# Pre-layernorm attention with a quantised linear layer: the first layernorm moved to other places and turned by VectorE and DMAs

## The chip, the cores and the metric

The kernel runs on one NeuronCore of a Trainium2 chip. Five engines with queues of their own share the work: PE (TensorE, matrix products and transposes, results in PSUM), DVE (VectorE), ACT (ScalarE), POOL (GpSimd) and SP (SyncE, which here only issues DMAs). Every DMA of the kernel is issued on SP's queue. The metric is the device time of one execution in microseconds, lower is better. The kernel before takes 774.85 us, the median of three runs (774.77 to 775.24).

## The reference, cut to what matters

There are 16 sequences of 256 tokens with 256 features, all float32. For each sequence:

```python
def layernorm(x):  # over the features, no scale, no shift
    return (x - mean(x)) / sqrt(var(x) + 1e-5)

h = layernorm(x)                      # "first layernorm"
q, k, v = h @ wq.T, h @ wk.T, h @ wv.T   # 16 query heads, 4 key/value heads, width 128
s = q @ k.T / sqrt(128)               # masked: a window of 32 and 4 sink tokens
x = x + softmax(s) @ v @ wo.T
h = layernorm(x)                      # "second layernorm"
hq = clip(round(h / scale), -128, 127)   # scale = max|h| / 127 for each token
x = x + (hq @ weight_q.T) * scale * weight_scale + bias
```

Matrix products need the features of `h` on the partitions, and the layernorm leaves the tokens there. So both layernorms are followed by a transpose.

## The kernel before, in words

**Slots.** The attention is cut into 128 units `(n, g, t)`: sequence, key/value head (with its four query heads), half of the tokens. The main loop goes over slots, one unit in each and two more at the end; eight slots make a sequence (`PER`). In a slot, PE makes the scores of the slot's unit (`pss`, L527), part of the output projection of an earlier unit (`py`, L645), the weighted values of the unit two slots back (`po`, L590), in every other slot a quarter of the next sequence's keys or values (`pk`, `pv`), and a pair of its query heads (`pq`, L494). Products of blocks are made with seven instead of eight matmuls, so sums of blocks are needed as factors: `os` of the attention's output and `xs` of the turned layernorm, both on POOL. Slots are named below by their place in a sequence: slot s is s modulo 8.

**Order.** The order in which instructions stand on each engine is the order in which the program writes them (`in_written_order`, L21). Small steps are hung on slots with `at(slot, f)` (L790) and run at the end of their slot. An instruction whose input is late thus holds back all that is written behind it on its engine, SP's DMA queue included.

**Weights of the attention.** After the softmax, VectorE turns the weights in blocks of 32 by 32 (`z`, L549), a DMA writes them to DRAM (`zd`, L551), and at the start of the next slot another brings them back in the wanted order (`ad`, L555); `po` two slots after the unit reads them. So `ad` has a little over one slot to be issued and to land.

**First layernorm.** `norm_steps` (L357) has three steps: statistics (`statistics`, L178: two instructions per half on DVE, two small ones on POOL, L187 and L188), and the two halves of the standardisation (L193, DVE). Then `turned` (L368) makes four PE transposes of 128x128 into PSUM (`xt`, L373), a DVE copy to `xnT` (L374), and POOL's four sums `xs` (`right_sums`, L263 to L266). Lines 807 to 813 hang these on four consecutive slots: statistics in slot 6, halves in slots 7 and 0, `turned` in slot 1, which is seven slots before the sequence begins; its `x` is loaded in slot 4. The first sequence has a function of its own, the second uses early slots.

**Second layernorm.** `ffn_steps` (L662) has six steps: `stats`, `norm` (with the bias added to x on POOL), `scale`, `quantise`, `turn` (a DMA transpose to `hT`, L695) and `linear` (four bf16 matmuls, L708; DVE scaling, L713; POOL addition, L714; the output's DMA, L715). They sit in slots 4, 5, 6, 0, 1 and 2 after their sequence (L834 to L840). The last but one sequence has them in slots 4 to 9 of the last sequence (the last two of these slots come after the last unit), and adds its bias inside `linear`. The last sequence is finished by `last_steps(0)` and `last_steps(1)` (L719), a half of the tokens each, at the very end.

**Values.** `values_to` (L412) lays values out for the window in one of three buffers, taken in rotation (L406 to L410).

**Weights.** Sums of blocks of the output weights (`output_weight_sums`, POOL) are made in slots 9 to 12 of the first two sequences, and the steps that quantise the linear layer's weights (`ffn_weight_steps`) in slots 5, 6, 8, 9, 10 and 11.

Of the kernel before, what the change touches and what calls it, by code (L numbers as in the profile page):

```python
# [9 lines left out]
FP = mybir.dt.float32  # L10
BF = mybir.dt.bfloat16
# [23 lines left out]
def kernel(  # L35
# [12 lines left out]
    pe, dve, act, pool, sp = nc.tensor, nc.vector, nc.scalar, nc.gpsimd, nc.sync  # L48
    B, T, DM = x.shape
    P = 128  # L50
    D = 128
# [3 lines left out]
    NC = DM // P  # L55
    NT = T // P
# [4 lines left out]
    QB = 32  # L61
    NBLK = P // QB
    SB = T // QB
# [5 lines left out]
    NKP = NCH * QB  # L69
# [1 line left out]
    SCALE = 1.0 / math.sqrt(D)  # L71

    const = ctx.enter_context(tc.tile_pool(name="const", bufs=1))
    xp = ctx.enter_context(tc.tile_pool(name="xp", bufs=4))
    p1 = ctx.enter_context(tc.tile_pool(name="p1", bufs=1))
    p2 = ctx.enter_context(tc.tile_pool(name="p2", bufs=2))
    p3 = ctx.enter_context(tc.tile_pool(name="p3", bufs=3))
    dram = ctx.enter_context(tc.tile_pool(name="dram", bufs=3, space=bass.MemoryType.DRAM))
# [12 lines left out]
    def load_x(n):  # L91
        if n < B:
            xts[n] = xp.tile([P, NT, DM], FP, tag="x", name=f"x_{n}")
            sp.dma_start(xts[n], x_v[n])
# [16 lines left out]
    bias_bc = const.tile([P, DM], FP, name="bias_bc")  # L111
# [138 lines left out]
    def fast_queries(n, h=0):  # L250
        return n > 0 and (n, h) != (B - 1, H - 2)
# [10 lines left out]
    def right_sums(t, b11, b12, b21, b22):  # L262
        pool.tensor_sub(t[0], b12, b11)  # L263
        pool.tensor_sub(t[1], b22, t[0])
        pool.tensor_sub(t[2], b22, b12)
        pool.tensor_sub(t[3], b21, t[1])  # L266
# [67 lines left out]
    xns, xnT, qt, kt, vw, xn_sums, mvs = {}, {}, {}, {}, {}, {}, {}  # L334
# [19 lines left out]
    def xn_blocks(n):  # L354
        return [[xnT[n][:, c, j * P : (j + 1) * P] for j in range(NT)] for c in range(NC)]

    def norm_steps(n):  # L357
# [7 lines left out]

        return [stats, lambda: norm(0), lambda: norm(1)]

    def turned(n):  # L368
        xnT[n] = p2.tile([P, NC, T], FP, tag="xnT", name=f"xnT_{n}")
        pt = ps_m.tile([P, NC, T], FP, tag="m", name=f"xt_{n}")  # L370
        for c in range(NC):
            for j in range(NT):
                pe.transpose(pt[:, c, j * P : (j + 1) * P], xns[n][:, j, c * P : (c + 1) * P], ident)  # L373
        dve.tensor_copy(xnT[n], pt)  # L374
        if fast_queries(n):
            xn_sums[n] = p2.tile([P, 4, P], FP, tag="xs4", name=f"xs4_{n}")
            b = xn_blocks(n)
            right_sums([xn_sums[n][:, i] for i in range(4)], *b[0], *b[1])

    def first_sequence():  # L380

# [22 lines left out]

    vws = [const.tile([NKP, SB, 2 * D], FP, name=f"vw_{j}") for j in range(3)]

    def values_buffer(n, pair):
        vw[n, pair] = vws[(2 * n + pair) % 3]  # L410

    def values_to(n, pair, v, tiles=range(NT)):  # L412


        w, fresh = vw[n, pair], 2 * n + pair < 3
        b0, b1 = tiles[0] * NBLK, (tiles[-1] + 1) * NBLK
        sp.dma_start(w[1:NKP:NCH, b0:b1], v[b0:b1].rearrange("b k d -> k b d"))
        c1 = min(b1 + 1, SB)
        sp.dma_start(w[0:NKP:NCH, b0 + 1 : c1], v[b0 : c1 - 1].rearrange("b k d -> k b d"))
        if b0 == 0:  # L420
            rows = QB if fresh else SINK
            sp.dma_start(w[2 : NCH * (rows - 1) + 3 : NCH], v[0, 0:rows].unsqueeze(1).to_broadcast([rows, SB, 2 * D]))
            if fresh:
                sp.dma_start(w[0:NKP:NCH, 0], v[0])
# [189 lines left out]
    def output_weight_sums(g):  # L614
        t = [wo_sums[:, i, 2 * g : 2 * g + 2] for i in range(4)]
        right_sums(t, *(wo_half(g, p, half) for p in range(2) for half in range(2)))
# [45 lines left out]
    def ffn_steps(n):  # L662
        xt = xts[n]
        tiles, tag = range(NT), f"{n}"
        h = p1.tile([P, NT, DM], FP, tag="h", name=f"h_{tag}")
        h16 = p1.tile([P, NT, DM], BF, tag="h16", name=f"h16_{tag}")
        xs = p2.tile([P, NT], FP, tag="xs", name=f"xs_{tag}")
        hT = p1.tile([P, NT, NC, P], BF, tag="hT", name=f"hT_{tag}")
        y = p1.tile([P, NT, DM], FP, tag="yo", name=f"y_{tag}")
        got = []  # L670

        def stats():
            got.append(statistics(xt, tiles, f"f{tag}"))

        def norm():
            standardise(h, xt, got[0], tiles)
            if n < B - 2:
                add_bias()

        def scale():  # L680
            dve.tensor_reduce(xs, h, AX.X, ALU.max, apply_absolute_value=True)
            dve.tensor_scalar(xs, xs, 1.0 / 127.0, 1e-12, ALU.mult, ALU.max)

        def quantise():
            xr = p2.tile([P, NT], FP, tag="xr", name=f"xr_{tag}")
            dve.reciprocal(xr, xs)
            for j in tiles:
                dve.scalar_tensor_tensor(
                    h[:, j, :], h[:, j, :], xr[:, j : j + 1], magic.to_broadcast([P, DM]), ALU.mult, ALU.add
                )  # L690
            pool.tensor_scalar(h, h, MAGIC + 127.0, MAGIC - 128.0, ALU.min, ALU.max)
            pool.tensor_scalar(h16, h, MAGIC, None, ALU.subtract)

        def turn():
            sp.dma_start_transpose(  # L695
                hT.rearrange("p j c t -> p (j c) t"), h16.rearrange("p j d -> p (j d)")
            )

        def add_bias():
            pool.tensor_add(xt, xt, bias_bc.unsqueeze(1).to_broadcast([P, NT, DM]))  # L700

        def linear():
            if n == B - 2:
                add_bias()
            pa = ps_m.tile([P, NT, DM], FP, tag="m", name=f"pa_{tag}")
            for j in tiles:
                for c in range(NC):
                    pe.matmul(  # L708
                        pa[:, j, :], hT[:, j, c], wqfT[:, c, :],
                        start=(c == 0), stop=(c == NC - 1),  # L710
                    )
            for j in tiles:
                dve.scalar_tensor_tensor(y[:, j, :], pa[:, j, :], xs[:, j : j + 1], wsc_bc, ALU.mult, ALU.mult)  # L713
            pool.tensor_add(y, y, xt)  # L714
            sp.dma_start(out_v[n], y)  # L715

        return [stats, norm, scale, quantise, turn, linear]

    def last_steps(j):  # L719

# [2 lines left out]
        n, tag = B - 1, f"last_{j}"  # L723
# [3 lines left out]
        y = p1.tile([P, NT, DM], FP, tag="xn", name=f"y_{tag}")[:, 0]  # L727
        mv = p2.tile([P, nc.vector.BN_AGGR_DIM], FP, tag="mv2", name=f"mv_{tag}")
        top, by, xs, least = (p2.tile([P, 1], FP, tag=k, name=f"{k}_{tag}") for k in ("top", "by", "xs1", "least"))
        hT = p1.tile([P, NT, NC, P], BF, tag="hT", name=f"hT_{tag}")[:, 0]  # L730

        def stats():
            st = p2.tile([P, nc.vector.BN_STATS_DIM], FP, tag="st2", name=f"st_{tag}")
# [45 lines left out]
    PER = G * NT  # L779
# [5 lines left out]
    def lag(i):  # L785
        return 2 if FIRST <= i < TAIL else 1

    chunks, early, asked, shares, small = {}, {}, {}, {}, {}

    def at(slot, f, what=small):  # L790
        what.setdefault(slot, []).append(f)
# [13 lines left out]
        for slot, h in zip(q, range(0, H, 2)):  # L805
            at(n * PER + slot, (n, h), asked)
    for n in range(1, B):
        first = n * PER - 10
        places = (first, first + 1, first + 2, first + 3) if n > 1 else (0, 1, 1, 2)
        for k, slot in enumerate(places[:3]):  # L810
            at(slot, lambda n=n, k=k: norm_steps(n)[k]())
        at(places[3], lambda n=n: turned(n))
        at(max(first - 2, 0), lambda n=n: n > 1 and load_x(n))
    for i, (n, g, t) in enumerate(units):
        if n == 0:
            at(i + 2 + lag(i), lambda u=(n, g, t): projected(*u), shares)
# [8 lines left out]
    at(1, lambda: weight_sums(wk_sb, wk_sums))  # L825
    for g in range(G):
        at((2, 4, 6, 8)[g], lambda g=g: weight_sums(wq_sb[:, :, g * HG * D : (g + 1) * HG * D], wq_sums[:, g]))
        at(9 + g, lambda g=g: output_weight_sums(g))
    at(0, other_loads)
    for slot, f in zip((5, 6, 8, 9, 10, 11), ffn_weight_steps()):  # L830
        at(slot, f)
    steps = {}
    for n in range(B - 1):
        done = (n + 1) * PER  # L834
        for k, slot in enumerate((4, 5, 6, 8, 9, 10) if n < B - 2 else (4, 5, 6, 7, 8, 9)):
            def step(n=n, k=k):
                if k == 0:
                    steps[n] = ffn_steps(n)
                steps[n][k]()
            at(done + slot, step)  # L840


    warm = ps_m.tile([P, P], FP, tag="m", name="warm")
# [14 lines left out]
    def get(i):  # L858
        return units[i] if 0 <= i < len(units) else None

    waiting, later, ways = None, {}, {}
    def values_now(i):
        return [times_values(*units[j]) for j in (i - 2, i - 1) if get(j) and j + lag(j) == i]

    def small_steps(i):
        for f in small.pop(i, []):
            f()

    for i in range(len(units) + 2):
        if i > len(units):  # L870
            small_steps(i)
        u, w = get(i), get(i - 1) if lag(i - 1) == 1 else None
        chunk = chunks.pop(i, [None])[0]
        nmax = scores_and_turned(u, w)
        if i - 1 in ways:
            ways.pop(i - 1)()
        if waiting:
            waiting.first()
        shared = shares.pop(i, [])
# [11 lines left out]
        waiting = None  # L891
# [33 lines left out]
        for f in combined:  # L925
            if f:
                f()
        if i == len(units) - 1:
            tail = last_steps(0)
            for f in tail[:2]:  # L930
                f()
# [38 lines left out]
```

## Time and profile before

| What | Value |
|---|---|
| runs | 774.85, 775.24, 774.77 us |
| the profiled execution: its own time | 774.85 us |
| its span (first to last instruction) | 773.1 us |
| time outside the span | 1.75 us |
| mean granted TensorE clock | 0.996 |
| busy: PE / DVE / POOL / ACT | 760.6 / 617.5 / 511.2 / 399.2 us |
| PE's transposes for the first layernorm (L373) | 60 matmuls, 9.0 us busy, 15 sequences |
| DVE's copies behind them (L374) | 15, 692 ns each |

Times in the profile are microseconds from the span's start, `x8` is a number of instructions, and brackets give the idle time ahead of an instruction and what ended it. Neighbouring matmuls overlap, so PE's busy time is no measure of a matmul's cost; the distance from one group's start to the next is. `PEld` is the load of the stationary operand, `SPq` the issue of a DMA.

### The profile page before, as it was taken

To read this page: it belongs to the slowest core of one execution; us is meant where nothing else is said; L and a number is where in the kernel's file an instruction comes from. 1 tells how busy PE (TensorE), PEld (TensorE's weight loads), DVE (VectorE), ACT (ScalarE), POOL (GpSimd) and SP (SyncE) were. 2 spreads that over 40 slices of the span, in tenths; PEclk is the share of its full clock that TensorE was granted. 3 is DMA by queue.
4 is the path that set the end of the run, shared out by engine and by line. 5 is a ranking of instruction groups with operands and counts; after the bars stand their busy time and mean duration, and the time that the engine had idled before them with its cause. 6 is when DMAs were issued, how large, how long until landed. Compare 5 with 4: busy or idle time off the path is not lost.

```text
span 773.1 us, 18754 instructions
## 1 busy us (share of the span) xinstructions
PE 760.6 (98%) x6539; PEld 748.1 (97%) x6539; DVE 617.5 (80%) x1774; ACT 399.2 (52%) x1561; POOL 511.2 (66%) x813
## 2 busy tenths in 40 slices
PE   9999999999999999999999999999999999999995
PEld 7999999999999999999999999999999999999993
DVE  2577888888888888888888888888888878878766
ACT  3655455455455454545555455554545555455551
POOL 4667967776765866767676666767667677676614
PEclk9999999999999999999999999999999999999998
DMA  7634334334343334434334343334434334343311
GB/s 243 197 100 113 120 110 124 105 95 137 118 138 109 106 103 120 141 113 123 101 96 141 110 141 105 104 115 120 130 114 127 97 106 141 103 134 105 99 35 34
DMA packets 113329, 90.34 MB, mean 117 GB/s; under 512 B 14548, under 2 KB 111444, under 8 KB 113236
## 3 DMA queue, kind: packets, MB, share of 16 engines
q1 hardware_dynamic: 113236, 89.16, 37.8%
q8 instruction: 52, 0.85, 0.5%
q14 instruction: 41, 0.34, 0.1%
HBM read 50.99 MB, written 36.18 MB: 113 GB/s over the span
## 4 chain that ended last, share of the span: by engine, by line
PE 95%; DVE 3%; ACT 0%; issue 0%; POOL 0%; DVEq 0%; POOLq 0%; ACTq 0%
PE pq L494 24%; PE py L645 23%; PE po L590 14%; PE pss L527 14%; PE pk L464 6%; PE pv L474 6%; PE py L629 3%; PE pq L505 2%; PE pa L708 1%; PE xt L373 1%; PE warm L845 1%; PE pv L439 0%; PE pk L430 0%; PE ptd L532 0%; ACT scores L565 0%
## 5 line engine op out<-in xcount | busy, mean ns | idle before, releaser
L565 ACT ACTIVATE scores<-scores,nmax 128x68 f32<-128x68 f32 x512 | 173.5, 340 | 254.3 <-DVE nmax L540 251.5
L590 PE MATMUL po<-ad,vw 96*128 96x128 f32 x1024 | 135.5, 275 | 0.0
L527 PE MATMUL pss<-kt,qt 128*128 128x68 f32 x1024 | 130.2, 268 | 0.0
L590 PEld LDWEIGHTS po<-ad,vw 96*128 96x128 f32 x1024 | 125.4, 192 | 1.6 <-ACT ad L535 0.7
L527 PEld LDWEIGHTS pss<-kt,qt 128*128 128x128 f32 x1024 | 126.1, 192 | 0.7 <-issue 0.5
L494 PE MATMUL pq<-xs,wq_sums 128*128 128x128 f32 x714 | 118.6, 275 | 0.0
L538 DVE SCALAR_TENSOR_TENSOR scores<-pss,masks 128x272 f32<-128x272 f32 x128 | 56.3, 440 | 67.7 <-PE pss L527 66.2
L494 PEld LDWEIGHTS pq<-xs,wq_sums 128*128 128x128 f32 x714 | 98.8, 192 | 0.0
L565 ACT ACTIVATION_READ_ACCUMULATOR scores<-scores,nmax 128x1 f32 x512 | 95.6, 187 | 0.0
L602 ACT COPY oT<-po 128x512 f32<-128x512 f32 x129 | 75.4, 585 | 22.6 <-PE po L590 22.6
L645 PE MATMUL py<-wo_sums,os 128*128 128x128 f32 x672 | 87.0, 279 | 0.0
L645 PEld LDWEIGHTS py<-wo_sums,os 128*128 128x128 f32 x672 | 79.5, 192 | 0.0
L304 POOL TENSOR_TENSOR ktmp<-b_k 128x256 f32<-128x256 f32 x30 | 24.6, 820 | 83.0 <-ACT b_k L325 83.0
L549 DVE STREAM_TRANSPOSE z<-scores 128x384 f32<-128x384 f32 x120 | 69.4, 578 | 4.1
L494 PE MATMUL pq<-xnT,wq_sb 128*128 128x128 f32 x476 | 72.6, 275 | 0.0
L257 POOL TENSOR_TENSOR os<-oT 128x256 f32<-128x256 f32 x56 | 41.2, 735 | 47.4 <-ACT oT L602 47.4
L494 PEld LDWEIGHTS pq<-xnT,wq_sb 128*128 128x128 f32 x476 | 62.7, 192 | 0.0
L645 PE MATMUL py<-wo_sb,oT 128*128 128x128 f32 x448 | 62.0, 281 | 0.0
L304 POOL TENSOR_TENSOR vt<-b_v 128x256 f32<-128x256 f32 x30 | 21.9, 729 | 57.8 <-ACT b_v L325 57.8
L540 DVE TENSOR_REDUCE nmax<-scores 128x4 f32<-128x272 f32 x128 | 55.8, 436 | 4.4
L584 DVE TENSOR_TENSOR scores<-scores,sm 128x272 f32<-128x272 f32 x120 | 55.2, 460 | 4.1
L645 PEld LDWEIGHTS py<-wo_sb,oT 128*128 128x128 f32 x448 | 54.5, 192 | 0.0
(184 smaller groups left out, 1740.9 us busy)
## 6 DMA issues: line engine op xcount, KB each, us to landing
zd<-z SPq DMA_DIRECT2D x120, 192.0 KB
ad<-zd SPq DMA_DIRECT2D x120, 192.0 KB
vw<-vd SPq DMA_DIRECT2D x31, 256.0 KB
vd<-vt SPq DMA_DIRECT2D x30, 256.0 KB
vw<-vd SPq DMA_DIRECT2D x30, 224.0 KB
x<-in_x_dram SPq DMA_DIRECT2D x15, 256.0 KB
out_dram<-y SPq DMA_DIRECT2D x15, 256.0 KB
wq_sb<-in_wqT_dram SPq DMA_DIRECT2D x4, 512.0 KB
```

The costliest lines, as they stand in the source:

```text
L304: eng.tensor_add(c11_u, like(p[0][:, 0:2], c11_u), two(p1, c11_u))
L464: pe.matmul(to, left, right, start=True, stop=True)
L494: pe.matmul(to, left, right, start=True, stop=True)
L527: pe.matmul(pss[:, k, :], qt[n, g][:, t, k].rearrange("p h i -> p (h i)"), kt[n, g][:, t * NBLK + k, :], start=True, stop=True,)
L538: dve.scalar_tensor_tensor(s[:, :, 0:NK], pss, SCALE, masks[:, t], ALU.mult, ALU.add)
L540: dve.tensor_reduce(nmax, s[:, :, 0:NK], AX.X, ALU.max, negate=True)
L549: dve.transpose(z, s.rearrange("p k (c i) -> p c k i", c=NCH))
L565: act.activation(s[:, k, 0:NK], s[:, k, 0:NK], AF.Exp, bias=nmax[:, k : k + 1], scale=1.0, accum_out=sm[:, k : k + 1],)
L584: dve.tensor_mul(s, s, sm.unsqueeze(2).to_broadcast([P, NBLK, NK]))
L590: pe.matmul(po[:, k], vw[n, g // 2][:, t * NBLK + k, g % 2 * D : (g % 2 + 1) * D], ad[:, :, k], start=True, stop=True,)
L602: act.copy(o[:, t, hs].rearrange("p h (k i) -> p k h i", i=QB), po[:, :, hs])
L645: pe.matmul(region(py, i), left[:, e], right[:, e], start=(g == 0 and e == 0 and i in (1, 4)), stop=(g == G - 1 and e == 1 and i in (7, 3)),)
```

## The change

1. **First layernorm, from the third sequence on.** The PE transposes are replaced by `turned_by_blocks`: DVE turns all 32x32 blocks in one instruction (128x512), four DMAs write the blocks to DRAM in pieces of 512 bytes (`out`), and four more bring them back to `xnT` in pieces of 128 bytes (`back`). POOL's sums become a function of their own (`channels`). The second sequence keeps `turned`.
2. **Places.** Statistics move from slot 6 to slot 2, the halves from slots 7 and 0 to slots 4 and 6, the DVE transpose comes in slot 7, `out` in slot 0 and `back` in slot 1, right after `ad` (the new list `begin`), and the sums at the end of slot 1, as before. The third sequence uses slots 4 to 9. `x` is loaded in slot 0, four slots earlier than before, and has five buffers instead of four.
3. **Last but one sequence.** `quantise` joins `scale` in the seventh slot of the last sequence, and its DMA transpose, bias (now on DVE) and `linear` all come in the eighth: the transpose at its start, `linear` just ahead of the first part of `last_steps(0)` (the new list `close`). `last_steps` takes its turned tile from two buffers of its own, and the extra call of the small steps in the slots after the last unit goes.
4. **Values.** Two buffers, one for each pair of heads, instead of three in rotation.
5. **Weights.** The last block sum of the output weights moves from slot 12 to slot 14; the linear layer's weight steps to slots 6, 9, 10, 10, 11 and 12.

```diff
-    xp = ctx.enter_context(tc.tile_pool(name="xp", bufs=4))
+    xp = ctx.enter_context(tc.tile_pool(name="xp", bufs=5))
...
+    def channels(n):
+        xn_sums[n] = p2.tile([P, 4, P], FP, tag="xs4", name=f"xs4_{n}")
+        b = xn_blocks(n)
+        right_sums([xn_sums[n][:, i] for i in range(4)], *b[0], *b[1])
...
+    def turned_by_blocks(n):
+        z = p1.tile([P, NQ, NT * NC, QB], FP, tag="zx", name=f"zx_{n}")
+        dve.transpose(z, xns[n].rearrange("p t (c q i) -> p q (t c) i", c=NC, q=NQ))
+        zd = dram.tile([P, NQ, NT * NC, QB], FP, tag="zx", name=f"zxd_{n}")
+
+        def out():
+            for a in range(NQ):
+                sp.dma_start(
+                    zd[:, a].rearrange("(q j) k i -> j q (k i)", q=NQ),
+                    z[a * QB : (a + 1) * QB].rearrange("j q k i -> j q (k i)"),
+                )
+
+        def back():
+            xnT[n] = p2.tile([P, NC, T], FP, tag="xnT", name=f"xnT_{n}")
+            for t in range(NT):
+                for c in range(NC):
+                    sp.dma_start(
+                        xnT[n][:, c, t * P : (t + 1) * P].rearrange("p (a i) -> p a i", a=NQ), zd[:, :, t * NC + c]
+                    )
+
+        return out, back
...
-    vws = [const.tile([NKP, SB, 2 * D], FP, name=f"vw_{j}") for j in range(3)]
+    vws = [const.tile([NKP, SB, 2 * D], FP, name=f"vw_{j}") for j in range(2)]
...
-        vw[n, pair] = vws[(2 * n + pair) % 3]
+        vw[n, pair] = vws[pair]
...
-        return [stats, norm, scale, quantise, turn, linear]
+        return [stats, norm, scale, quantise, turn, linear, lambda: add_bias(dve)]
...
-        hT = p1.tile([P, NT, NC, P], BF, tag="hT", name=f"hT_{tag}")[:, 0]
+        hT = p2.tile([P, NC, P], BF, tag="hT1", name=f"hT_{tag}")
...
-        first = n * PER - 10
-        places = (first, first + 1, first + 2, first + 3) if n > 1 else (0, 1, 1, 2)
+        first = n * PER - 14
+        places = (0, 1, 1, 2) if n == 1 else (4, 5, 6, 7) if n == 2 else (first, first + 2, first + 4, first + 5)
...
+            def turn(n=n, slot=places[3]):
+                for k, f in enumerate(turned_by_blocks(n)):
+                    at(slot + 1 + k, f, begin)
+                at(slot + 2, lambda: channels(n))
...
-        at(9 + g, lambda g=g: output_weight_sums(g))
+        at((9, 10, 11, 14)[g], lambda g=g: output_weight_sums(g))
...
-    for slot, f in zip((5, 6, 8, 9, 10, 11), ffn_weight_steps()):
+    for slot, f in zip((6, 9, 10, 10, 11, 12), ffn_weight_steps()):
...
-        for k, slot in enumerate((4, 5, 6, 8, 9, 10) if n < B - 2 else (4, 5, 6, 7, 8, 9)):
+        slots = (4, 5, 6, 8, 9, 10) if n < B - 2 else (4, 5, 6, 6, 7, 7, 7)
+        for k, slot in enumerate(slots):
...
-            at(done + slot, step)
+            at(done + slot, step, begin if k == 4 and n == B - 2 else close if k == 5 and n == B - 2 else small)
```

More of the change, by code (lines that the diff above doesn't have):

```diff
@@ L374, in turned @@
         dve.tensor_copy(xnT[n], pt)
[L375 to L378, printed above, removed]
+        channels(n)
+    def turned_by_blocks(n):
[16 more added lines that the diff above has]
+        return out, back
+    NQ = P // QB
     def first_sequence():
@@ L402, in keys_to @@
         act.copy(k[:, :, :, 2 * QB :], kb[:, :, 0, 0:SINK].unsqueeze(2).to_broadcast([P, 2, SB, SINK]))
-    vws = [const.tile([NKP, SB, 2 * D], FP, name=f"vw_{j}") for j in range(3)]
+    vws = [const.tile([NKP, SB, 2 * D], FP, name=f"vw_{j}") for j in range(2)]
     def values_buffer(n, pair):
-        vw[n, pair] = vws[(2 * n + pair) % 3]
+        vw[n, pair] = vws[pair]
     def values_to(n, pair, v, tiles=range(NT)):
-        w, fresh = vw[n, pair], 2 * n + pair < 3
+        w, fresh = vw[n, pair], n == 0
         b0, b1 = tiles[0] * NBLK, (tiles[-1] + 1) * NBLK
@@ L677, in norm @@
             if n < B - 2:
-                add_bias()
+                add_bias(pool)
         def scale():
@@ L697, in turn, with add_bias @@
             )
-        def add_bias():
-            pool.tensor_add(xt, xt, bias_bc.unsqueeze(1).to_broadcast([P, NT, DM]))
+        def add_bias(eng):
+            eng.tensor_add(xt, xt, bias_bc.unsqueeze(1).to_broadcast([P, NT, DM]))
         def linear():
-            if n == B - 2:
-                add_bias()
             pa = ps_m.tile([P, NT, DM], FP, tag="m", name=f"pa_{tag}")
@@ L786, in lag @@
         return 2 if FIRST <= i < TAIL else 1
-    chunks, early, asked, shares, small = {}, {}, {}, {}, {}
+    begin, close, chunks, early, asked, shares, small, later = {}, {}, {}, {}, {}, {}, {}, {}
     def at(slot, f, what=small):
@@ L807 @@
     for n in range(1, B):
-        first = n * PER - 10
-        places = (first, first + 1, first + 2, first + 3) if n > 1 else (0, 1, 1, 2)
+        first = n * PER - 14
+        places = (0, 1, 1, 2) if n == 1 else (4, 5, 6, 7) if n == 2 else (first, first + 2, first + 4, first + 5)
         for k, slot in enumerate(places[:3]):
             at(slot, lambda n=n, k=k: norm_steps(n)[k]())
-        at(places[3], lambda n=n: turned(n))
-        at(max(first - 2, 0), lambda n=n: n > 1 and load_x(n))
+        if n == 1:
+            at(places[3], lambda n=n: turned(n))
+        else:
+            def turn(n=n, slot=places[3]):
+                for k, f in enumerate(turned_by_blocks(n)):
+                    at(slot + 1 + k, f, begin)
+                at(slot + 2, lambda: channels(n))
+            at(places[3], turn)
+            at(max(first - 2, 0), lambda n=n: load_x(n))
     for i, (n, g, t) in enumerate(units):
@@ L859, in get @@
         return units[i] if 0 <= i < len(units) else None
-    waiting, later, ways = None, {}, {}
+    waiting, ways = None, {}
     def values_now(i):
@@ L869 @@
     for i in range(len(units) + 2):
-        if i > len(units):
-            small_steps(i)
         u, w = get(i), get(i - 1) if lag(i - 1) == 1 else None
@@ L876 @@
             ways.pop(i - 1)()
+        for f in begin.pop(i, []):
+            f()
         if waiting:
@@ L928 @@
         if i == len(units) - 1:
+            for f in close.pop(i):
+                f()
             tail = last_steps(0)
```

## The prediction

> **What bounds the kernel now.** I read the shares of the engines, then the chain of waits, then PE's idle time by stage, then PE, DVE, POOL and SP row by row in one sequence from the middle. First the page's engine line, the chain's shares and windows of the start, the middle and the end (columns: window, length, busy PE, PEld, DVE, ACT, POOL, granted clock, DMA share, GB/s).
>
> ```profile
> PE 760.6 (98%) x6539; PEld 748.1 (97%) x6539; DVE 617.5 (80%) x1774; ACT 399.2 (52%) x1561; POOL 511.2 (66%) x813
> ...
> PE 95%; DVE 3%; ACT 0%; issue 0%; POOL 0%; DVEq 0%; POOLq 0%; ACTq 0%
> ...
> 95.00:142.00 47.00, 45.67 (x409) 45.43 (x408) 39.59 (x115) 24.48 (x97) 32.86 (x51) 1.00 0.37 113
> 420.00:467.00 47.00, 47.00 (x423) 46.91 (x421) 39.46 (x115) 24.93 (x99) 32.41 (x50) 1.00 0.38 116
> 734.00:773.00 39.00, 30.19 (x192) 26.03 (x191) 25.34 (x73) 13.67 (x48) 10.45 (x17) 0.92 0.13 36
> ```
>
> The reader is to see that PE has no gap in the middle at a full clock, 1.33 us of gap in the window from 95, and 9 us at the end. So in the middle, time goes only if PE work goes, and comes if something makes PE wait. A sequence takes 46.55 us (`py` of the same slot: 404.72, 451.26, 497.82). In the sequence used below, slot 0 starts at 478.30, slot 1 at 484.55, slot 2 at 490.12, slot 3 at 496.81, slot 4 at 501.95 (first `pss`).
>
> **The change part by part.** *PE's transposes.* On PE's timeline:
>
> ```profile
> 489.46 0.39 PE L494 MATMUL pq<-xnT,wq_sums 128*128 128x128 f32 x2
> 489.69 0.60 PE L373 MATMUL xt<-ident,xn 128*128 128x128 f32 x4
> 490.12 1.01 PE L527 MATMUL pss<-kt,qt 128*128 128x68 f32 x8
> ```
>
> From the start of `xt` to the next group's start are 0.43 us. Fourteen of the 15 sequences lose it: 14 x 0.43 = **-6.0 us**, all on the path.
>
> *VectorE.* The copy of 0.69 us goes from slot 1; the transpose of 128x512 comes in slot 7, by the row nearest to it (`z`, a transpose of 128x384 in 0.578) an estimated 0.578 x 512/384 = 0.77. There a half of the standardisation (0.39) leaves, so DVE gets 0.38 more against 0.86 idle ahead of L538. Slot 4 receives a half (0.39, idle 1.15), slot 2 the statistics (0.92, idle 1.64). Nothing reaches PE: 0, and were one cover gone, at most the excess over its idle time, which no row shows.
>
> *A stall at the start goes.* PE waits 1.33 us at 97.56 for DVE's `qt`. DVE stood at `h` (idle 1.12, then 1.60 busy) for POOL's `mv_f`, and POOL made the last block sum of the output weights first (90.08 to 93.2):
>
> ```profile
> 92.26 0.93 POOL L266 TENSOR_TENSOR wo_sums<-wo_sb,wo_sums 128x256 f32<-128x256 f32 x1
> 93.28 0.22 POOL L187 TENSOR_SCALAR mv_f<-mv_f 128x2 f32<-128x2 f32 x1
> 94.33 1.60 DVE L193 TENSOR_SCALAR h<-x,mv_f 128x256 f32<-128x256 f32 x2 [1.12 <-POOL mv_f L188]
> 97.56 0.46 PE L474 MATMUL pv<-wv_sb,xs 128*128 128x128 f32 x2 [1.33 <-DVE qt L305]
> ```
>
> That sum (3.1) moves to slot 14; a weight step (0.61) and a sequence's statistics (0.99) come onto POOL ahead instead. So `mv_f` ends some 3.1 - 1.6 = 1.5 us earlier, before DVE is free for `h` at 93.22. The 1.12 leave DVE, and **-1.2 us** on PE (bounds -1.33 and 0, if another wait takes its place). The remaining 0.81 us stall of the start (slot 6, at 48.68) has none of these instructions before it and stays.
>
> *What the moved statistics delay.* They issue two POOL instructions, 0.22 at L187 and 0.71 at L188; with the 0.06 between, 0.99 us. In slot 2 POOL has them now ahead of the addition that ends the second layernorm's product, L714. Behind L714 stands the output's DMA on SP's queue, and behind that `ad` of slot 3:
>
> ```profile
> 498.66 1.27 POOL L714 TENSOR_TENSOR y<-y,x 128x512 f32<-128x512 f32 x1
> ...
> 521.98 0.22 POOL L187 TENSOR_SCALAR mv_a<-mv_a 128x2 f32<-128x2 f32 x1
> 522.28 0.71 POOL L188 TENSOR_TENSOR mv_a<-mv_a,half 128x2 f32<-128x2 f32 x1
> ...
> 498.73 0.37 SPq L479 DMA_DIRECT2D vd<-vt  x1
> 499.95 0.39 SPq L715 DMA_DIRECT2D out_dram<-y  x1
> 500.45 0.41 SPq L555 DMA_DIRECT2D ad<-zd  x1
> ...
> 504.07 0.97 PEld L590 LDWEIGHTS po<-ad,vw 96*128 96x128 f32 x8
> ```
>
> SP issues `out_dram` when the addition ends, `ad` 0.50 later, `ad` lands at 503.23 (the last completion in the trace), and PE loads its first block at 504.07: 0.84 us of slack. Over the twelve sequences from the third to the fourteenth the slacks are 0.97, 1.03, 0.96, 1.10, 1.02, 0.81, 0.89, 1.00, 0.84, 1.01, 0.81 and 0.59. An `ad` that came just in time showed 0.10 between landing and load. So each sequence loses 0.99 + 0.10 minus its slack, in sum **+2.1 us**. Bounds: 0 (slot 2 starts 0.43 earlier after its neighbour's transposes went, and if POOL runs ahead of PE by that much all of it is covered) and +6 (0.50 in each, the worst slack every time).
>
> *SP's queue and `back`.* In slot 0 SP issues four `out` behind `vw` and `ad`, at 0.60 each by the `vw` rows, so the next `zd` moves from 483.32 to about 484.5 and slot 1's `ad` from 485.26 to about 486.4; its slack in the other sequences is 1.7 to 1.9, so 0.6 remain. Then come the four `back`: 2048 pieces of 128 bytes, 128 for each of the 16 rings. They start when `ad`'s packets end, at about 488.6. No row has pieces of data that small. The two nearest: `hT` moves 256-byte pieces at 24 ns each on a ring (512 of them in 0.78 us), and `ad` 512-byte pieces from DRAM at 46 to 48 (384 in 1.1 to 1.2). So `back` takes 3.1 to 6.1 us and has landed (0.4 for the completion) between 492.1 and 495.1. Then POOL makes the sums `xs`:
>
> ```profile
> 492.23 0.47 POOL L263 TENSOR_TENSOR xs<-xnT 128x128 f32<-128x128 f32 x1
> 495.68 0.73 POOL L304 TENSOR_TENSOR vt<-b_v 128x256 f32<-128x256 f32 x1 [1.62 <-ACT b_v L325]
> ```
>
> The four last 1.84 us. Behind them on POOL stands the combination of the values, L304, which can start at 495.25 (0.43 earlier, as PE). So `back` may land until 493.4 at no cost, which is 34 ns a piece. I take 24: a packet's own duration goes down with its size in this trace (27 ns for 512 bytes, 18 for 256, 9 for 4), so 128 bytes stand nearer to the 256-byte row: **0**. At 48 it would be 495.1 + 1.84 - 495.25 = 1.7 us a sequence.
>
> The Trainium skill speaks against this: its page "DMA: Bandwidth & Descriptors", section Specifications, gives 512 B as the smallest transfer at line rate, with a read-modify-write below. In this trace the 256-byte pieces were quicker than the 512-byte ones; no run shows 128. If the rule doubled the slower pitch, an estimate by that page is 12 us for `back`, and a sum of 769.0 + 12 x 7.9, about 864 us.
>
> *Loads and buffers.* With two value buffers the writer must wait for the product that read them one sequence before, three slots earlier: 0. `x` has one buffer more for a load four slots earlier: 0. The third sequence's `x` now stands ahead of the output weights; their first quarter, landed at 30.48, comes 0.75 to 1.1 later, against PE's need at 32.0: 0. If one of these were not covered it would cost its lateness once, under 1.
>
> *The end.* On DVE and PE:
>
> ```profile
> 762.24 0.87 DVE L713 SCALAR_TENSOR_TENSOR y<-pa,xs,wsc_bc 128x256 f32<-128x256 f32 x2
> 762.38 1.03 PE L629 MATMUL py<-wo_sb,oT 128*128 128x256 f32 x4
> 763.53 1.25 DVE L766 TENSOR_TENSOR y_last<-y_last,x_last 128x256 f32<-128x256 f32 x1
> 764.71 0.42 DVE L734 BATCH_NORM_STATS2 st_last<-py 128x6 f32<-128x256 f32 x1
> ```
>
> The last half's statistics start at 764.71 though their `py` ended at 763.41: DVE was busy with L713 and with L766, which took 1.25 where its twin later takes 0.42, with POOL's L714 running. After the change L713 and L714 come before `last_steps(0)`. Its statistics go from 756.45 to about 757.8, its `d_last` ends at 761.6 instead of 760.6, the last `py` at 763.87 (+0.46), L766 takes 0.42, and the last half's statistics start at 764.0: **-0.7 us**. Bounds: -1.3 (they start as `py` ends, as before) and +1.33 (the shift of the first half passes through whole).
>
> *Sum.* 774.85 (the profiled execution; 773.1 of span and 1.75 around it; it is also the median of the runs) - 6.0 - 1.2 + 2.1 - 0.7 = **769.0 us**.
>
> **The rivals.** *A, `ad` isn't late.* POOL waits for ACT and PE in slots 1 and 2 (1.62 idle ahead of L304), so it may regain the 0.43 in each sequence; against it, 18.0 us of SP's idle time end on this very addition. 769.0 - 2.1 = 766.9. *B, slower: `back` is too slow.* POOL's `xs` come late, the value combination behind them, `vd`, `out_dram` and `ad` behind it, with no slack left. From 34 ns a piece each further ns costs 128 x 0.001 x 12 = 1.5 us; break-even with before at 38; at `ad`'s 48 the time is 769.0 + 12 x 1.7 = 789.4. For it: `ad` also comes from DRAM, and its 46 ns are more than its packets' own 27. Against it: `hT`. *C, the end gets longer.* The path from L713 over the first half's statistics holds the end as a whole: +1.33 instead of -0.7, 771.0.
>
> **How the numbers follow.** Forecast 0.52, A 0.16, C 0.08, B 0.24. The forecast's own bounds and A and C lie between 766.2 and 771.2, which is 0.76; four hundredths more come from B between 34 and 40 ns, up to 777. A run can tell 0.2%, 1.55 us, from no change. Faster: 0.52 + 0.16 + 0.08, less 0.02 for costs left open, 0.74; the same 0.04, half of it B near break-even; slower 0.22.
>
> **What would show it.** No L373 rows from the third sequence on; `py` to `py` 46.1 to 46.4 us in place of 46.55; PE's gap near 97 gone; PE idle 0.1 to 0.5 us ahead of the `po` of slot 3, put down to `ad` or SP; POOL's statistics directly ahead of L714; `back`'s pieces at 20 to 34 ns on a ring, and POOL's first `xs` by 493; the last statistics within 0.7 us of the last `py`. I am wrong if POOL idles at `xs` for the DMA and a sequence takes over 46.55 us, or if `po` waits in a slot other than 3.

## The result and the profile after

The changed kernel takes 780.23 us (780.06 to 781.29, four runs) against 775.05 us (774.77 to 775.32) for the kernel before on the same chip. The ratio is 1.007, with an interval of 1.0052 to 1.0087: it is slower by 5.2 us. The forecast was 769.0 us. The profiled execution of the changed kernel has a span of 778.5 us, 5.4 more than before's 773.1.

The page of the changed kernel: the engines' busy time, the shares of the chain that ended last, and one window from the middle (columns as in the prediction).

```profile
PE 758.6 (97%) x6483; PEld 744.0 (96%) x6483; DVE 624.7 (80%) x1775; ACT 399.4 (51%) x1561; POOL 512.7 (66%) x812
...
PE 86%; DVE 11%; issue 2%; ACT 0%; POOL 0%; DVEq 0%; POOLq 0%; ACTq 0%
...
424.00:471.00 47.00, 46.29 (x413) 45.99 (x412) 39.40 (x114) 24.31 (x98) 32.04 (x50) 1.00 0.44 127
```

PE has lost its 56 transposes, as it should. But the window that had no gap before now has 0.71 us of one, at a full clock, and VectorE has 11% of the chain where it had 3%. PE's list of waits (waiting engine and line, releaser, us in total, times, longest) names it:

```profile
PE py L674 <- DVE pc L305: 8.5, 12, 0.7
PE ht_last L784 <- DVE d_last L779: 3.1, 2, 2.9
```

Twelve times PE waits for `pc`, VectorE's first steps in combining the output projection. They read the banks in PSUM that the next group of `py` is to overwrite. The wait lies in slot 4 of every sequence from the third to the fourteenth. Here it is in the sequence whose slot 3 starts at 500.21 (before: 496.81), first PE, then VectorE, then POOL, all in the changed kernel:

```profile
505.35 1.01 PE L556 MATMUL pss<-kt,qt 128*128 128x68 f32 x8
507.06 1.13 PE L674 MATMUL py<-wo_sb,oT 128*128 128x128 f32 x8 [0.71 <-DVE pc L305]
...
503.74 0.71 DVE L601 TENSOR_TENSOR sm<-sm,floor 128x4 f32<-128x4 f32 x1
504.49 0.18 DVE L602 RECIPROCAL sm<-sm 128x4 f32<-128x4 f32 x1
504.70 0.97 DVE L613 TENSOR_TENSOR scores<-scores,sm 128x272 f32<-128x272 f32 x1
506.62 0.29 DVE L305 TENSOR_TENSOR pc<-py,pc 128x128 f32<-128x128 f32 x1
...
502.48 0.72 POOL L188 TENSOR_TENSOR mv_a<-mv_a,half 128x2 f32<-128x2 f32 x1
503.17 1.27 POOL L741 TENSOR_TENSOR y<-y,x 128x512 f32<-128x512 f32 x1
504.65 0.73 POOL L257 TENSOR_TENSOR os<-oT 128x256 f32<-128x256 f32 x1 [0.21 <-ACT oT L631]
```

The same in the kernel before, first PE, then the three steps of VectorE (POOL's L714 is shown in the prediction):

```profile
501.95 1.01 PE L527 MATMUL pss<-kt,qt 128*128 128x68 f32 x8
502.79 1.11 PE L645 MATMUL py<-wo_sb,oT 128*128 128x128 f32 x8
...
500.34 0.16 DVE L572 TENSOR_TENSOR sm<-sm,floor 128x4 f32<-128x4 f32 x1
...
500.75 0.44 DVE L584 TENSOR_TENSOR scores<-scores,sm 128x272 f32<-128x272 f32 x1
...
502.15 0.29 DVE L305 TENSOR_TENSOR pc<-py,pc 128x128 f32<-128x128 f32 x1
```

Two VectorE instructions of unchanged shape became longer, from 0.16 to 0.71 and from 0.44 to 0.97 us. Both take two inputs from SBUF. The first ends at 504.45, as POOL's addition L741 ends (503.17 + 1.27 = 504.44). The second ends 0.29 us after the end of POOL's next instruction (504.65 + 0.73 = 505.38, against 505.67). That VectorE wasn't working in that time, though the profile counts it as busy, but was held while POOL ran, is shown by the runs below. Counted from the start of slot 3, `pc` at L305 comes at 6.41 us instead of 5.34, which is 1.07 late. PE's `py` starts 1.71 us after `pss` instead of 0.84, so it loses 0.87, and the groups after it lose 0.20 more. A sequence takes 47.18 us instead of 46.55, where the prediction had 46.1 to 46.4.

The difference between the two traces can be followed from unit to unit, by the first weight load of each unit's `po`:

| Where | Before to after, us |
|---|---|
| from the start to the first `po` | +0.4 |
| slots 3 to 15, without the transposes | -1.2 |
| 14 sequences without PE's transposes, 0.43 to 0.44 each | -6.1 |
| slot 4 of 12 sequences, 0.99 up to `po` and 0.08 behind it | +12.8 |
| from slot 3 of the last but one sequence to the end | -0.5 |
| sum | +5.4 |

The +0.4 arises in PE's first product of the values, which takes 2.39 us in place of 1.98 though PE doesn't wait in it. The clock record of this trace has the full clock from 7.00 us on, that of before from 5.81, and those of the other versions from 4.3 to 7.4. So this row is a matter of the single execution and not of the change.

### The profile page after: what moved, and what is told of

Read it like the earlier page. It is cut to its first block, busy times and chain, and to the rows that moved or that the text cites. A ratio compares the mean times of both kernels' runs of the same rounds, so it can differ in the third digit from the quotient of the medians.

```text
span 778.5 us, 18824 instructions
## 1 busy us (share of the span) xinstructions
PE 758.6 (97%) x6483; PEld 744.0 (96%) x6483; DVE 624.7 (80%) x1775; ACT 399.4 (51%) x1561; POOL 512.7 (66%) x812
## 4 chain that ended last, share of the span: by engine, by line
PE 86%; DVE 11%; issue 2%; ACT 0%; POOL 0%; DVEq 0%; POOLq 0%; ACTq 0%
PE pq L523 21%; PE py L674 21%; PE po L619 13%; PE pss L556 11%; PE pk L493 6%; PE pv L503 6%; PE py L658 3%; DVE scores L613 2%; PE pq L534 2%; DVE y L740 1%; DVE sm L601 1%; PE pa L735 1%; DVE nmax L569 1%; DVE scores L567 1%; DVE qt L306 1%
## 5 line engine op out<-in xcount | busy, mean ns | idle before, releaser
L613 DVE TENSOR_TENSOR scores<-scores,sm 128x272 f32<-128x272 f32 x120 | 61.5, 513 | 4.1
```

What stands on the lines that cost most here:

```text
L613: dve.tensor_mul(s, s, sm.unsqueeze(2).to_broadcast([P, NBLK, NK]))
```

## The experiments

**The theories.** P, a read port that two engines share: the statistics' two POOL instructions push the addition L741 by 1.1 us, so that it runs when VectorE reaches its two instructions with both inputs in SBUF; these wait for POOL. Q: `ad` of slot 3 comes late, as the prediction had it. R: the new DMAs slow something. The Trainium skill, page "SBUF — State Buffer", section "Who interferes with whom", states a rule that fits P: a VectorE instruction with two SBUF inputs and a GpSimd instruction that reads SBUF contend for a shared read interface, and the second to start waits until the first is through; one that only writes doesn't contend.

**Statistics in slot 1.**

```diff
-        places = (0, 1, 1, 2) if n == 1 else (4, 5, 6, 7) if n == 2 else (first, first + 2, first + 4, first + 5)
+        places = (0, 1, 1, 2) if n == 1 else (4, 5, 6, 7) if n == 2 else (first - 1, first + 2, first + 4, first + 5)
```

> The changed kernel with one place altered: the statistics of the first layernorm stand in slot 1 instead of slot 2, from the third sequence on. Theory P (port): the statistics' two POOL instructions push L741, the addition of x, by 1.1 us; VectorE's two instructions with both inputs in SBUF (the maximum with the floor, L601, and the scaling of the weights, L613) then meet POOL instructions that read SBUF and wait for their ends, the combination of the output projection (pc) is 1.07 us late, and PE waits for it ahead of slot 4's projection. In slot 1 POOL has 1.17 us of idle time for the 0.99 and VectorE 0.89 for the 0.92, so the wait goes: 780.2 - 12 x 1.07 = 767.4 us (766 to 769), L601 and L613 of slot 3 at 0.16 and 0.44 us. Theory Q (the step of the prediction: ad of slot 3 late): also about 767, since ad is issued 1 us earlier. Theory R (the new DMAs slow VectorE or the loads): 780, unchanged.

Measured: 768.11 us (768.08 to 768.36), ratio to before 0.9912 (0.9897 to 0.9927). In the trace PE has no wait in slot 4, and VectorE's two instructions of slot 3 are short again:

```profile
495.21 0.17 DVE L601 TENSOR_TENSOR sm<-sm,floor 128x4 f32<-128x4 f32 x1
...
495.63 0.44 DVE L613 TENSOR_TENSOR scores<-scores,sm 128x272 f32<-128x272 f32 x1
```

So the place of the statistics is what costs, and R falls. P and Q both expected this; the next two part them.

**The output's DMA behind `ad`.**

```diff
-            sp.dma_start(out_v[n], y)
+            if n < B - 2:
+                at((n + 1) * PER + 11, lambda: sp.dma_start(out_v[n], y), begin)
+            else:
+                sp.dma_start(out_v[n], y)
```

> The changed kernel, with the output's DMA issued in slot 3 behind the load of the weights (ad) instead of ahead of it; the order on POOL and VectorE is as in the changed kernel. Theory P: ad comes about 1 us earlier and its slack ahead of po in slot 4 grows from 0.8 to about 1.5 to 2, but the time stays at 780.2 (779.4 to 781.0), with PE's 0.71 us of idle time ahead of slot 4's py in twelve sequences. Theory Q: the lateness of ad is what costs, and the time falls to 767 to 770.

Measured: 780.32 us (779.89 to 780.74), the same as the changed kernel. `ad`'s slack ahead of slot 4's `po` rose from mostly 0.7 to 0.9 us to 2.6 to 3.3, more than expected, and PE's wait didn't move:

```profile
PE py L674 <- DVE pc L305: 8.6, 12, 0.7
```

Taking the lateness of `ad` away gains nothing while PE's wait stands, so Q falls as the cause.

**Memsets in place of POOL's addition.**

```diff
-            pool.tensor_add(y, y, xt)
+            if n < B - 2:
+                pool.memset(y, 0.0)
+                pool.memset(y, 0.0)
+            else:
+                pool.tensor_add(y, y, xt)
```

> The changed kernel, with POOL's addition of x to the linear layer's product (L741) replaced by two memsets of the same tile, of nearly the same length together (2 x 0.56 against 1.27 us), which write SBUF and read nothing; so this kernel leaves out the linear layer's result in the output of all but the last two sequences. POOL's order, the output's DMA and the late ad stay. Theory P: VectorE's instruction with two SBUF inputs (L601 in slot 3) takes 0.16 instead of 0.71 us, the scaling (L613) is through before POOL's next instruction, PE's wait in slot 4 goes: 767 to 769 us. Theory Q: ad is as late as before, 779 to 781. Theory R: 780.

Measured: 767.75 us (767.04 to 768.96), ratio 0.9909 (0.9892 to 0.9925). POOL, then VectorE, then PE's weight load:

```profile
494.09 0.53 POOL L742 MEMSET y<- 128x512 f32 x1
494.67 0.52 POOL L743 MEMSET y<- 128x512 f32 x1
...
494.67 0.16 DVE L601 TENSOR_TENSOR sm<-sm,floor 128x4 f32<-128x4 f32 x1
...
495.08 0.44 DVE L613 TENSOR_TENSOR scores<-scores,sm 128x272 f32<-128x272 f32 x1
...
498.40 0.97 PEld L619 LDWEIGHTS po<-ad,vw 96*128 96x128 f32 x8
```

POOL is busy at the same moment, but with instructions that read nothing, and L601 takes 0.16. For this pair of instructions that is the page's rule, shown in this kernel. The run also prices Q alone. Here `ad` landed at 498.34, 0.06 before the load, and in the other sequences 0.04 to 0.09 before it. Against the kernel before (0.84 in this sequence) most of the slack was gone. The load came up to 0.13 us later than in the versions where `ad` has slack, but one slot on eleven of the twelve sequences had lost 0.02 us or less: a weight load runs ahead of its matmuls, and that lead took up the delay. The twelfth lost 0.5, and 0.3 of that is also there with the statistics in slot 1. The memsets are together some 0.2 us shorter than the addition, so the price of the full lateness isn't shown by this run; it lies above 0 by 0.2 us a sequence at most.

**The statistics' place alone, in the kernel before.**

```diff
-        places = (first, first + 1, first + 2, first + 3) if n > 1 else (0, 1, 1, 2)
+        places = (0, 1, 1, 2) if n == 1 else (first - (4 if n > 2 else 0), first + 1, first + 2, first + 3)
...
-        at(max(first - 2, 0), lambda n=n: n > 1 and load_x(n))
+        at(max(first - (6 if n > 2 else 2), 0), lambda n=n: n > 1 and load_x(n))
```

> The kernel before, with one part of the change alone: from the third or fourth sequence on the statistics of the first layernorm stand in slot 2 (x loaded four slots earlier, five buffers for it), its halves, the PE transposes and all else stay. Theory P: a wait of PE in slot 4 in twelve sequences, L572 and L584 of slot 3 at 0.7 and 0.95 us instead of 0.16 and 0.44: 775.0 + 12 x 1.07 = 787.9 us, and if VectorE's second instruction comes just ahead of POOL's next one, not less than 775.0 + 12 x 0.4 = 780. Theory Q: 775.0 + 2.1 = 777.1. Theory R: 775, since no DMA of the new path is there.

Measured: 789.40 us (788.46 to 790.18), ratio 1.0186 (1.0170 to 1.0201). One of the change's places, put into the old kernel, costs 14 us. POOL and VectorE show the same two meetings:

```profile
510.79 1.26 POOL L714 TENSOR_TENSOR y<-y,x 128x512 f32<-128x512 f32 x1
512.27 0.73 POOL L257 TENSOR_TENSOR os<-oT 128x256 f32<-128x256 f32 x1 [0.21 <-ACT oT L602]
...
511.36 0.72 DVE L572 TENSOR_TENSOR sm<-sm,floor 128x4 f32<-128x4 f32 x1
...
512.33 0.97 DVE L584 TENSOR_TENSOR scores<-scores,sm 128x272 f32<-128x272 f32 x1
```

Its trace puts 12 x 1.08 us into slot 4. The rest, about 2.4 us by the trace, comes from the start, where one wait is longer (2.22 us of gap in place of 1.33 near 98) and PE's granted clock is then 0.50 in the window from 98.10 to 101.40, where it was 1.00 before.

**Only the statistics' POOL part behind the addition.**

```diff
-        eng.tensor_scalar(mv[:, js, 1], mv[:, js, 1], LN_EPS, None, ALU.add)
-        pool.tensor_tensor(mv[:, js, 1], mv[:, js, 1], half[:, js], ALU.pow)
+        def root():
+            eng.tensor_scalar(mv[:, js, 1], mv[:, js, 1], LN_EPS, None, ALU.add)
+            pool.tensor_tensor(mv[:, js, 1], mv[:, js, 1], half[:, js], ALU.pow)
...
+        if slot:
+            at(slot, root, trail)
+        else:
+            root()
```

The new list `trail` runs behind all small steps of its slot.

> The changed kernel, with the statistics' two POOL instructions (0.22 and 0.72 us, 128x2) moved behind L741, the addition of x, and VectorE's part of the statistics left where it is. POOL then makes the addition 1 us earlier, the output's DMA and ad of slot 3 come on time. Theory P: the small instruction L188 now runs when VectorE reaches L601 (the maximum with the floor) and holds it as long as the addition did, up to about 0.5 us, and L613 then meets the next block sum: PE's wait in slot 4 stays, 779 to 781 us; if the small instruction doesn't hold VectorE, 767 to 768. Theory Q (ad late): 767 to 768.

Measured: 767.46 us (767.36 to 767.94), ratio 0.9906 (0.9891 to 0.9921): faster than both kernels. My first branch was wrong, the second held. POOL's small instruction runs beside both of VectorE's and holds neither:

```profile
494.47 0.72 POOL L189 TENSOR_TENSOR mv_a<-mv_a,half 128x2 f32<-128x2 f32 x1
...
494.50 0.18 DVE L607 TENSOR_TENSOR sm<-sm,floor 128x4 f32<-128x4 f32 x1
...
494.93 0.44 DVE L619 TENSOR_TENSOR scores<-scores,sm 128x272 f32<-128x272 f32 x1
```

So a POOL instruction that reads SBUF doesn't hold VectorE for its whole time in every case, as the page's rule would have it: this one, with two elements for each partition, took 0.72 us and lengthened the maximum by 0.04 at most over the twelve sequences. The kernel before has a longer case in slot 1, POOL's L692 with one input:

```profile
487.90 1.50 POOL L692 TENSOR_SCALAR h<-h 128x512 bf16<-128x512 f32 x1
...
488.08 0.45 DVE L572 TENSOR_TENSOR sm<-sm,floor 128x4 f32<-128x4 f32 x1
...
488.77 0.44 DVE L584 TENSOR_TENSOR scores<-scores,sm 128x272 f32<-128x272 f32 x1
```

The maximum is longer there, but ends 0.87 us ahead of POOL's instruction, and the scaling keeps its 0.44. Moving POOL's part alone settles one rival more: VectorE's part of the statistics stays in slot 2, so its 0.92 us aren't what makes PE wait.

**PE's transposes back, all else as changed.**

```diff
-            def turn(n=n, slot=places[3]):
...
-            at(places[3], turn)
+            at(places[3] + 2, lambda n=n: turned(n))
```

> The changed kernel with part 1 undone: PE transposes in slot 1 in place of VectorE's transpose and the eight DMAs; all other places stay. Theories P and Q: PE gets 14 x 0.43 = 6.0 us back, the wait in slot 4 stays: 780.2 + 6.0 = 786.3 us (785.5 to 787). Theory R (the new DMAs cause the wait): the wait goes, 780.2 + 6.0 - 12.8 = 773.4.

Measured: 786.22 us (785.76 to 786.73), ratio 1.0147 (1.0132 to 1.0162), 6.0 us above the changed kernel. The twelve waits stay (8.5 us in PE's list). The transposes' price is confirmed, and with none of the new DMAs the wait is there all the same.

**The weight steps back in their old slots.**

```diff
-        at((9, 10, 11, 14)[g], lambda g=g: output_weight_sums(g))
+        at(9 + g, lambda g=g: output_weight_sums(g))
-    for slot, f in zip((6, 9, 10, 10, 11, 12), ffn_weight_steps()):
+    for slot, f in zip((5, 6, 8, 9, 10, 11), ffn_weight_steps()):
```

> The changed kernel with part 5 undone: the weight steps in the slots of the kernel before (9 to 12 and 5, 6, 8, 9, 10, 11). The traces of before and after differ by -1.25 us up to slot 15; if the weight steps' places make that difference, 780.2 + 1.25 = 781.5 us (781 to 782.5) with a wait of about 1.3 us or more near 97 us; if the earlier x load or the new places of the third sequence made it, 780.2.

Measured: 786.20 us (784.72 to 787.14), ratio 1.0145 (1.0130 to 1.0160): 6.0 us, not 1.25. There are two causes. Near 101 it is the one that the prediction had named, VectorE's `h` waiting for POOL's `mv_f`, and the gap is larger than before's 1.33. Near 50 VectorE has both the weight step (L207 to L209, 47.77 to 48.85) and the first half of the third sequence's standardisation (0.89 at 46.96) ahead of slot 6's scores. VectorE, PE, and PE's clock in the window behind the gap (the third column from the right):

```profile
98.25 1.60 DVE L193 TENSOR_SCALAR h<-x,mv_f 128x256 f32<-128x256 f32 x2 [1.68 <-POOL mv_f L188]
...
101.47 0.46 PE L503 MATMUL pv<-wv_sb,xs 128*128 128x128 f32 x2 [2.26 <-DVE qt L305]
...
102.79 1.06 PE L503 MATMUL pv<-wv_sums,xs 128*128 128x128 f32 x4
...
102.21:105.40 3.19, 3.19 (x19) 3.19 (x18) 2.96 (x8) 1.55 (x4) 0.90 (x3) 0.55 0.18 64
```

There are two such gaps, 2.18 us near 50 and 2.26 near 101. After each the granted clock falls to half for some 3 us (0.50 in the windows from 52 to 53 and 53 to 54, too). The traces differ by 2.6 us at the first and by 4.1 at the second, and by hardly anything elsewhere.

**The end as before.**

```diff
+            if n == B - 2:
+                add_bias(pool)
...
-        slots = (4, 5, 6, 8, 9, 10) if n < B - 2 else (4, 5, 6, 6, 7, 7, 7)
+        slots = (4, 5, 6, 8, 9, 10) if n < B - 2 else (4, 5, 6, 7, 8, 9)
...
```

> The changed kernel with part 3 undone: the last but one sequence's steps in slots 4 to 9, with the addition of the bias on POOL. From the last slots on the change gained about 0.5 us between the traces of before and after, where the prediction had 0.7: 780.2 + 0.5 = 780.7 us (780.2 to 781.2), all of it behind the last unit. If the two buffers of the turned tile were what gained, no difference (they stay).

Measured: 780.32 us (779.83 to 780.53), 0.1 above the changed kernel, which these runs can't tell from nothing. From slot 124 on the trace is 0.3 us longer. Part 3 is worth little.

**The third sequence's halves together.**

```diff
-        places = (0, 1, 1, 2) if n == 1 else (4, 5, 6, 7) if n == 2 else (first, first + 2, first + 4, first + 5)
+        places = (0, 1, 1, 2) if n == 1 else (4, 6, 6, 7) if n == 2 else (first, first + 2, first + 4, first + 5)
```

> A version that combines: the changed kernel with the statistics' two POOL instructions behind the addition of x (767.5 us when run alone), and the first half of the third sequence's standardisation moved from slot 5 to slot 6, since in the traces it stands on VectorE ahead of slot 6's scores (0.89 us at 46.3) and PE then waits 1.2 us for VectorE at 49. If that half is the cause, the wait falls to 0.3 us or less and the time to 766.3 us (765.8 to 767.0); if POOL's sums of the query weights, which hold VectorE's instructions with two SBUF inputs in slot 5 (0.55 and 0.84 us instead of 0.16 and 0.44), are the cause, 767.5 stays.

Measured: 767.35 us (767.09 to 767.64) against 767.46 without this edit, no difference that can be told. PE's wait of 1.2 us fell to 0.8, not to 0.3. In the trace 0.37 us are won at that place and kept to the end, which is less than the spread of the runs. Part of the wait is that half; the remainder wasn't settled.

## Why the prediction was wrong, point by point

The step that failed is "What the moved statistics delay". It saw that the two POOL instructions stand ahead of L714, and that 0.99 us pass on from there. It then followed the delay along one road only, SP's queue and `ad`, and priced that at +2.1. Along this road it came as computed (`ad` landed 1.15 us later in its slot), and it cost nothing that the runs could show; from the memsets it lies between 0 and 2.4 us in all. The range ended at 771.2, though this step's own bound of +6 would have given 772.9. What the step left out is that POOL's addition, once moved, runs at the same time as other VectorE instructions. That road cost 12 x 1.07 = 12.8 us. With 12.8 in place of 2.1, and the other terms at their measured size, the sum gives 774.85 - 6.1 - 1.2 - 0.5 + 12.8 = 779.9; the +0.4 of the start makes it the profiled execution's 780.3.

The evidence was in the trace of before. L714 ended at 499.93 and L572 began at 500.34, so a shift of 0.99 had to make them meet. One slot earlier in the same sequence the same L572 stood beside another POOL instruction with two inputs, took 0.42 instead of 0.16 us and ended 0.02 after it; so it was in twelve other places of the trace, at 0.40 to 0.42:

```profile
493.60 0.45 POOL L266 TENSOR_TENSOR xs<-xnT,xs 128x128 f32<-128x128 f32 x1
...
493.65 0.42 DVE L572 TENSOR_TENSOR sm<-sm,floor 128x4 f32<-128x4 f32 x1
```

And the prediction itself quoted L766 at 1.25 instead of 0.42 us "with POOL's L714 running", and used it for the end. The same POOL instruction runs in every sequence, and I didn't ask there what it would meet.

- *PE's transposes*: right, -6.1 for -6.0. Undoing them alone gave +6.0.
- *VectorE's covers*: right. The transpose of 128x512 took 0.67 us (estimate 0.77), and no wait of PE ends on it.
- *The stall at the start*: the mechanism is right. The gap at 97 is gone (-1.57 with what followed it), but that the other stall, of 0.81, stays, failed: it became 1.20. The prediction had found none of the moved instructions before it, but the weight step L207 to L209 stood there (46.01 to 47.06 in before). It left, and a half of the standardisation (0.89) came. That slots 3 to 15 still gave the forecast -1.2 is partly luck: the gap gave more than that, and the other stall took it back.
- *`back`*: right that it costs nothing. The trace has its 2048 pieces in 2.75 us in this sequence (2.5 to 3.9 in all), 21.5 ns each on a ring, where I took 24. But SP needs 2.61 us to issue the four DMAs, so that is the pace at which they were issued, and the rings may be quicker. POOL's `xs` began at 496.09, without any wait, behind the sums `os` that POOL was still making. The estimate of 12 us, twice `ad`'s 48 ns for each piece, that the prediction set beside the 512 B for line rate of the Trainium skill (page "DMA: Bandwidth & Descriptors", section Specifications) was far off.
- *The end*: right in its steps. The last half's statistics start 0.10 us after the last `py` ends (1.30 before), and L766's twin takes 0.42:

```profile
768.82 1.03 PE L658 MATMUL py<-wo_sb,oT 128*128 128x256 f32 x4
...
769.61 0.42 DVE L793 TENSOR_TENSOR y_last<-y_last,x_last 128x256 f32<-128x256 f32 x1
769.95 0.42 DVE L761 BATCH_NORM_STATS2 st_last<-py 128x6 f32<-128x256 f32 x1
```

  Between the two traces that is -0.5 of the -0.7. By the trace of the run with the end as before, part 3 holds 0.3 of it.
- *Loads and buffers*: no wait of PE names them.
- *The rivals*: none of the three came. A was right that `ad` would cost nothing, though `ad` was late. B had the right sign with the wrong mechanism, and its bound, 34 ns, was never reached (at most 31).
- *The signs*: the prediction looked for an idle PE ahead of the `po` of slot 3. The load that it measured, at 504.07, is that of slot 4, which starts at 501.95. PE did wait in slot 4, but ahead of `py`, and for VectorE.

## What to carry to other kernels

When an edit moves an instruction, ask of every later instruction on its engine not only who waits for it, but also what it will now run beside. In this kernel VectorE and POOL hold each other up without any semaphore between them, and the profile books the hold as busy time. POOL loses less: its sum L258 took 0.80 us in the twelve places where the scaling still ran as it began, and 0.72 to 0.73 in the other 44. A VectorE instruction whose duration differs between two places with the same shape (0.16 and 0.42 or 0.71 here) is the sign to look for: note what POOL does in that moment, and treat the distance to POOL's neighbouring instruction as a slack, like that of a DMA.

## What the hardware showed that I had not expected

- VectorE's small maximum (L601) waits for the whole rest of a POOL addition or subtraction of 128x512, 128x256 or 128x128, and then mostly ends 15 to 23 ns after it. The scaling of 128x272 ends 0.29 us after POOL's instruction, less than its own 0.44. It isn't held by a memset of 128x512, nor, for the whole time, by POOL's 128x2 instruction of 0.72 us or its TENSOR_SCALAR of 128x512 with one input (1.50 us). Why these are harmless wasn't tried; that the first reads so few elements, and the second only one input, is a guess.
- Gaps of PE of 2.18, 2.22 and 2.26 us were followed by some 3 us at a granted clock of 0.50, while gaps of 0.71, 1.20 and 1.33 us were followed by 1.00. By the mean clock it doesn't come each time: of the four executions of the kernel before with the statistics moved, two had 0.993 and took 790.1 to 790.2 us, two had 0.996 and took 788.5 to 788.7. The Trainium skill, page "TensorE: Matmul & The Clock Gate", in Part 1, puts the fall after an idle window of about 3.4 us; the gaps measured here were shorter. So a wait of 2 us can cost 4 on PE, as the one near 101 did.
- DMA pieces of 128 bytes from DRAM took at most 21.5 ns on a ring, less than the 46 of the 512-byte pieces; the profile's packets took 13 and 27 ns.
